# Edge lists read amid the second attention, root products behind it, and a front that works in node order

## The chip, the cores and the metric

The kernel runs on one core of a Trainium2 chip. The metric is the device time of one execution in microseconds (us). Before the change five executions took 2762.19 to 2769.22 us, with a median of 2766.24. Lower is better.

The core has four compute engines that run beside each other: TensorE (PE, matrix products), VectorE (DVE), ScalarE (ACT) and GpSimd (POOL). SyncE (SP) issues transfers. Indirect transfers (gathers and scatters of rows by an index list) are issued by POOL.

## The reference

A graph of 1250 nodes with 768 features and 20000 edges goes through two residual blocks. All is fp32.

```python
h = relu(layernorm(x))
# two GATv2 layers, 8 heads and then 1 head
fs = h @ Ws + bs ; fd = h @ Wd + bd
e = leaky_relu(fs[src] + fd[dst], 0.2)
alpha = softmax over the edges of one dst of einsum(e, attn)
out = elu(segment_sum(alpha * fs[src], dst))
# between them: h = layer_norm(out + h) * ln1_w + ln1_b
x = x + layer_norm(out of the second) * lno_w + lno_b

h = relu(layernorm(x))
# a relational layer over 34 edge types, then a graph convolution
seg = edge_type * n + dst
mean = segment_sum(h[src], seg) / max(count(seg), 1)
h1 = einsum('rni,rio->no', mean, W_rel) + h @ W_root + b_rgcn
xw = h1 @ W_gcn
dinv = rsqrt(deg + 1) ; norm = dinv[src] * dinv[dst]
x = x + segment_sum(xw[src] * norm, dst) + xw * dinv**2 + b_gcn
```

The edges arrive sorted by `dst`.

## The kernel before

**Order of the nodes.** Nodes are ranked by their number of incoming edges. A tile is 128 nodes of neighbouring rank; there are ten tiles (`NT`), and tile k has as many edge slots as its largest node needs (`CAPS[k]`, 33 in the first). A slot is one edge of each of the 128 nodes, so one indirect gather brings the 128 source rows of a slot. All slots of all tiles are 179.

**Front** (`fast_front`, L616 to L1076). It loads x, normalizes it, stores h (`f.h0_d`), and counts for each node where its edges begin in the sorted list (`got`, `first`, L777 to L829). `sources(j)` (L813 to L819) is the product h @ W1s of one block of rows; ten of them make the table `f.fs_d` that attention gathers from. Sort keys are spread over all partitions by products with `diag` (L859, L860); a comparison on DVE gives the `rank` (L865); ten scatters write the record (node, begin, degree) of each node to its rank's row (L880), and `rk` reads it back (L901). Then ten gathers fetch, for each rank, the window of the edge list that holds its edges (L912), and five select steps on DVE (L926 to L929) shift each window to its beginning; the result is `f.ell`. On PE's queue the shift product stands behind `sources(0)`, the key products behind `sources(1)`, and the others behind them.

`pairs` (`f.pairs`) computes for each edge how many edges of the same type its node has before it, and so which place the edge gets in the lists of the relations: DVE comparisons `same`, `cnt`, `early`, `turn` (L959 to L1030), counting products on PE (L970 to L979), a reduction over the partitions (`badc`, L1061, `fl_ps`, L1063), and `pick`/`pl` (L1024 to L1037). The places go to memory and come back as `f.place` (L1069, L1375).

**Attention** (`attention`, called twice). It works in chunks of up to 16 slots. `front(c, i)` gathers one slot into a ring of 24 buffers `fs` (L1148), optionally issues list scatters, and computes on DVE `z = max(fs, nfd)` (L1208), the product with the attention vector (L1213) and the sum per head (L1214); the one-head layer does the last two in one (L1210). `softmax` works on a chunk. `back` scales and sums the slots: with eight heads ACT scales (L1266) and PE adds with the identity (L1268), with one head ACT builds a diagonal matrix (L1256) and PE multiplies by it (L1258). While chunk j goes through `back`, chunk j+1 goes through `front`. At the end of a tile `end` divides, applies ELU and calls `finish`.

`list_edges` (called in `front`) issues scatters of the edge records into the lists `pair_d` of the relations (L1152), at 0.9 a slot from slot 16 of the first tile on, and 60 more at the last slot, or what is left of them. `negated1` gathers h of a tile, transposes it and multiplies it with W1d (L1116) for `nfd` (L1416). `finish1` normalizes, multiplies with the weights of the second layer (L1433, L1440) and scatters the table `fs2_d`. `finish2` normalizes, adds x, normalizes again, scatters h (`h2_d`), and computes the product with W_root, whose `root` rows (L1480) it scatters to `h1_d`.

**Relations.** After the second attention its pools are closed, and those of the relations opened. The lists are read (L1532), counts are made (L1536 to L1547, with one product, `more`, on PE), and then jobs run: `first_half` loads a relation's weights (L1159), gathers and sums the rows of its sources (`g`, `g2`, `g3`) and transposes them; `second_half` multiplies with the weights (L1116) and scatters with addition into `h1_d` (L1603). Beside that DVE writes an adjacency matrix (`arow`, L1511, L1513).

**Tail.** For some tiles the convolution is done by gathering and adding h1 rows (`acc`, `nb`, twelve buffers, L1665), for the others by products with the adjacency (L1674).

The order on each engine follows the program, save where `tc.issue_after` names an instruction that has to be issued first. A tile's buffer is waited for by its next user; a pool that is closed gives its memory to later pools, whose users wait for the last readers.

Of the kernel before, what the change touches and what calls it, by code (L numbers as in the profile page):

```python
# [18 lines left out]
P = 128  # L19
# [607 lines left out]
def fast_front(ctx, tc, f, x, src, dst, edge_type, W1s, b1s, W1d, b1d, attn1, attno, W_rel):  # L627
# [34 lines left out]
    rank_d = dram.tile([NP, 4], I32, name="f_rank_d")  # L662
# [9 lines left out]
    f.ell = keepp.tile([P, NT, S0], I32, name="f_ell")  # L672
# [4 lines left out]
    f.place_d = dram.tile([P, NT * S0], I32, name="f_place_d")  # L677
    f.w1d = const.tile([P, KC, D], F32, name="f_w1d")

    with ExitStack() as front:  # L680
# [110 lines left out]

        quarter = SLOPE / (1.0 - SLOPE)
# [29 lines left out]
        last = sources(0)  # L822
# [8 lines left out]
        with tc.issue_after(last.ins):  # L831
            last = nc.tensor.matmul(sh_ps[:, 0:1], shift, first[:, 0:1], start=True, stop=True)
        with tc.issue_after(last.ins):
            last = sources(1)
# [3 lines left out]


# [14 lines left out]
        with tc.issue_after(last.ins):  # L854
            for g in range(2):
                wide = ps_m.tile([P, 2, 512], F32, name="wide", tag="ag").rearrange("p a b -> p (a b)")
                for lo, hi in ((0, 512), (512, N // 2)):
                    at = slice(g * (N // 2) + lo, g * (N // 2) + hi)
                    nc.tensor.matmul(wide[:, lo:hi], ones16[:EP], flat2[:, at], start=True, stop=False)  # L859
                    last = nc.tensor.matmul(wide[:, lo:hi], big16[:EP], flat[:, at], start=False, stop=True)  # L860
                nc.scalar.copy(keys[:, g * (N // 2):(g + 1) * (N // 2)], wide[:, :N // 2])
# [7 lines left out]
        rec = prep.tile([P, NT, 4], I32, name="rec")  # L869
        nc.vector.memset(rec, 0)  # L870
        nc.vector.tensor_copy(rec[:, :, 0], node)
        nc.vector.tensor_copy(rec[:, :, 1], first[:, :NT])
        nc.vector.tensor_copy(rec[:, :, 2], deg)

        past = prep.tile([NP - N, 4], I32, name="past")
# [10 lines left out]
        with tc.issue_after(last_keys.ins):  # L886
            sources(2)


        packed = prep.tile([EP, EC], I32, name="packed")  # L890
        nc.vector.scalar_tensor_tensor(packed, ev[:, 2, :], 2048.0, ev[:, 0, :], op0=ALU.mult, op1=ALU.add)
        zrow = prep.tile([1, RW], I32, name="zrow")
        nc.vector.memset(zrow, 0)
        pk = packed.rearrange("p (r c) -> p r c", c=RW)
        nc.scalar.dma_start(win_d[1:NR + 1, :RW].rearrange("(p r) c -> p r c", p=EP), pk)
        nc.scalar.dma_start(win_d[0:NR, RW:].rearrange("(p r) c -> p r c", p=EP), pk)
        nc.scalar.dma_start(win_d[NR:NR + 1, RW:], zrow)


        rk = prep.tile([P, NT, 4], I32, name="rk")  # L900
# [3 lines left out]
        nc.vector.tensor_copy(f.degf, rk[:, :, 2])  # L904
        arow = prep.tile([P, NT], I32, name="arow")
        nc.vector.tensor_scalar(arow, rk[:, :, 1], 5, None, op0=ALU.arith_shift_right)
        nc.vector.tensor_scalar(arow, arow, float(NR - 1), 1.0, op0=ALU.min, op1=ALU.add)
        offs = prep.tile([P, NT], I32, name="offs")
        nc.vector.tensor_scalar(offs, rk[:, :, 1], RW - 1, None, op0=ALU.bitwise_and)
        win = prep.tile([P, NT, WIN], I32, name="win")  # L910
        for k in range(NT):
            nc.gpsimd.indirect_dma_start(  # L912
                out=win[:, k, :], out_offset=None, in_=win_d[:, :],
                in_offset=bass.IndirectOffsetOnAxis(ap=arow[:, k:k + 1], axis=0))
        wf = prep.tile([P, NT, WIN], F32, name="wf")
        nc.vector.tensor_copy(wf, win)
        bits = prep.tile([P, 5, NT], F32, name="bits")
        for i in range(5):
            bi = prep.tile([P, NT], I32, name="bi", tag="bi", bufs=2)
            nc.vector.tensor_scalar(bi, offs, i, 1, op0=ALU.arith_shift_right, op1=ALU.bitwise_and)  # L920
            nc.vector.tensor_copy(bits[:, i, :], bi)
        for i in (4, 3, 2, 1, 0):
            b = 1 << i
            L = S0 + b - 1
            df = prep.tile([P, NT, S0 + 15], F32, name="df", tag="df")
            nc.vector.tensor_sub(df[:, :, :L], wf[:, :, b:b + L], wf[:, :, :L])  # L926
            nc.vector.tensor_tensor(df[:, :, :L], df[:, :, :L],
                                    bits[:, i, :, None].to_broadcast([P, NT, L]), op=ALU.mult)
            nc.vector.tensor_add(wf[:, :, :L], wf[:, :, :L], df[:, :, :L])  # L929
        nc.vector.tensor_copy(f.ell, wf[:, :, :S0])  # L930
        nc.vector.tensor_scalar(f.srci, f.ell, 2047, None, op0=ALU.bitwise_and)
# [5 lines left out]
        def pairs():  # L937
# [13 lines left out]
            typ = pp.tile([P, NT, S0], I32, name="typ")  # L951
            nc.vector.tensor_scalar(typ, f.ell, 11, None, op0=ALU.arith_shift_right)
            tv = pp.tile([P, NT, S0], F16, name="tv")
            nc.vector.scalar_tensor_tensor(tv, pad, 100.0, typ, op0=ALU.mult, op1=ALU.add)
# [101 lines left out]
            pl_i = pp.tile([P, NT, S0], I32, name="pl_i")  # L1056
# [11 lines left out]
            nc.vector.scalar_tensor_tensor(pl_i, pad, float(P * COLS), pl, op0=ALU.mult, op1=ALU.add)  # L1068
            nc.sync.dma_start(f.place_d[:, :], pl_i.rearrange("p k s -> p (k s)"))  # L1069

        for j in range(3, NT):
            sources(j)
# [53 lines left out]
def fast_rest(ctx, tc, f, x, src, dst, edge_type, W1s, b1s, W1d, b1d, attn1, ln1_w, ln1_b,  # L1126
# [9 lines left out]
    h2_d = dram.tile([NP + P, D], F32, name="r_h2_d")  # L1136
    ZERO = NP + (PT + 1) * P
    h1_d = dram.tile([ZERO + 1, D], F32, name="r_h1_d")
    pair_d = dram.tile([P * f.COLS, 3], I32, name="r_pair_d")
# [11 lines left out]
    def scatter(table, rows, idx, group, **kw):  # L1151
        s = nc.gpsimd.indirect_dma_start(  # L1152
            out=table, out_offset=bass.IndirectOffsetOnAxis(ap=idx, axis=0), in_=rows, in_offset=None, **kw)
        tc.declare_no_dep(s.ins, group=group, reason="every node's row is written once")
        tc.add_to_no_dep_group(group, s.ins)

# [15 lines left out]
    def attention(H, table, negated, attn_e, first, loads, finish, rate, rest):  # L1172
# [21 lines left out]
        def front(c, i):  # L1194
# [5 lines left out]
            if s >= CHUNK or t.k:  # L1200
                list_edges(row, rate)
            if t.k == NT - 1 and s == t.S - 1:
                list_edges(row, rest)
            if t.lg is None:
                lg = pool.tile([P, S0 * f.H], F32, name="lg", tag="lg", bufs=2)
                t.lg = lg[:, :S0 * H].rearrange("p (s h) -> p s h", h=H)
# [116 lines left out]
        for j, now in enumerate(chunks):  # L1323
# [8 lines left out]
            if after:  # L1332
                softmax(after)
                if j + 2 == len(chunks):
                    for i in range(after.n):
                        back(after, i)
            if now.first + now.n == now.t.S:
                end(now.t)
# [10 lines left out]
    def prepare_lists():  # L1349
# [3 lines left out]
        with tc.tile_pool(name="r_fill", bufs=1, side="right") as fp:  # L1353
            lane = rp.tile([P, 1], F32, name="lane")
            nc.gpsimd.iota(lane, pattern=[[0, 1]], base=NP, channel_multiplier=1,
                           allow_small_or_imprecise_dtypes=True)
            fill = fp.tile([P, COLS, 3], I32, name="fill")
            nc.vector.memset(fill[:, :, 2], 0)
            ones_c = fp.tile([P, COLS], F32, name="ones_c")
            nc.vector.memset(ones_c, 1.0)  # L1360
            nc.vector.tensor_scalar(fill[:, :, 0], ones_c, lane, None, op0=ALU.mult)
            for t in range(PT + 1):
                cols = fill[:, :R * PC, 1].rearrange("p (r c) -> p r c", c=PC)[:, :, t] if t < PT else fill[:, R * PC:, 1]
                n = R if t < PT else PX
                nc.vector.tensor_scalar(cols, ones_c[:, :n], lane, float(t * P), op0=ALU.mult, op1=ALU.add)
            nc.vector.memset(fill[:, :R * PC, 1].rearrange("p (r c) -> p r c", c=PC)[:, :, PT:], 0)
            nc.sync.dma_start(pair_d.rearrange("(p c) f -> p c f", p=P), fill)
            zero = fp.tile([P, D], F32, name="zero")
            nc.vector.memset(zero, 0.0)
            nc.sync.dma_start(h2_d[NP:, :], zero)  # L1370
            for t in range(PT + 1):
                nc.sync.dma_start(h1_d[NP + t * P:NP + (t + 1) * P, :], zero)
            nc.sync.dma_start(h1_d[ZERO:, :], zero[:1])
        f.place = rp.tile([P, NT, S0], I32, name="place")
        nc.sync.dma_start(f.place, f.place_d.rearrange("p (k s) -> p k s", k=NT))  # L1375
# [21 lines left out]
    with ExitStack() as one:  # L1397
# [22 lines left out]
        def finish1(k, o):  # L1420
# [16 lines left out]
            scatter(fs2_d[:, :], fs, f.perm[:, k:k + 1], "fs2")  # L1437
# [6 lines left out]
        attention(H, f.fs_d, negated1, f.attn_1, prepare_lists, loads1, finish1, 0.9, 60)  # L1444
# [290 lines left out]
```

## Time and profile before

| What | us |
|---|---|
| median of five executions | 2766.24 |
| profiled execution, own time | 2764.64 |
| its span, first to last instruction | 2762.8 |
| front, to the first gather of h | 0 to 151.5 |
| first attention, first z to last table scatter | 183 to 884 |
| second attention, first gather to last sums | 888 to 1335 |
| last sums to the first relation product | 1335 to 1390 |
| relations | 1390 to 2561 |
| tail | 2561 to 2763 |

| Engine | busy us | share |
|---|---|---|
| PE | 2352.4 | 85% |
| DVE | 1566.3 | 57% |
| POOL | 1525.3 | 55% |
| ACT | 853.1 | 31% |

The mean granted TensorE clock was 0.933. The profile page shows one execution; its slices are 40 equal parts of the span, each digit the busy share in tenths. In the rows of the timeline the columns are start, busy time, engine, line, operation, output and inputs, and in brackets the idle time before it and what ended it. A busy share over the whole span hides the stages, so each stage is read by itself.

### The profile page before, as it was taken

The numbers are of one execution on the slowest core, as the hardware profiler recorded it, in microseconds if no ns is written. First come the engines' busy times: TensorE is split into PE (matmuls) and PEld (weight loads), VectorE is DVE, ScalarE is ACT, GpSimd is POOL, SyncE is SP. The second block draws the span as 40 slices with busy tenths as digits, with TensorE's granted clock in tenths as the row PEclk, the third lists the DMA queues.
The fourth block names the chain that finished last, engine by engine and source line by source line (L and its number), as shares of the span: only waits on it lengthen the run. The fifth ranks groups of instructions, "written<-read, shape, count | busy, mean of one in ns | idle before, by whom it ended". The sixth has DMA issues, their size and how long they took to land. (4 is left out here: it accounts for less than half of the span.)

```text
span 2762.8 us, 24188 instructions
## 1 busy us (share of the span) xinstructions
PE 2352.4 (85%) x7759; PEld 1364.5 (49%) x7759; DVE 1566.3 (57%) x2361; ACT 853.1 (31%) x2308; POOL 1525.3 (55%) x1113
## 2 busy tenths in 40 slices
PE   6953685788897486988699999999999999999688
PEld 3521243444454243544356666666666666665254
DVE  5599979998994999999362222222223232210262
ACT  3004766767862122333211112211212211222010
POOL 1343886878884776776275444444444454431471
PEclk8976897999998698999899999999999999999899
DMA  6155443445431776775387777777777777766783
GB/s 217 41 166 182 128 138 94 130 129 141 133 103 58 263 212 188 221 214 171 141 243 194 196 188 188 187 196 197 192 195 193 184 190 185 186 163 154 206 272 126
DMA packets 136549, 476.85 MB, mean 173 GB/s; under 512 B 26186, under 2 KB 28515, under 8 KB 136414
## 3 DMA queue, kind: packets, MB, share of 16 engines
q0 software_dynamic: 83712, 334.44, 46.8%
q1 hardware_dynamic: 48043, 134.21, 13.7%
q10 hardware_dynamic: 4658, 6.57, 0.7%
q8 instruction: 64, 1.05, 0.2%
q14 instruction: 72, 0.58, 0.1%
HBM read 385.91 MB, written 89.33 MB: 172 GB/s over the span
## 5 line engine op out<-in xcount | busy, mean ns | idle before, releaser
L1116 PE MATMUL ps<-wrel,mT 128*128 128x384 f32 x3336 | 1099.5, 486 | 1.5 <-DMA wrel<-in_L_gnn_W_rel_dram 1.5
L1116 PEld LDWEIGHTS ps<-wrel,mT 128*128 128x128 f32 x3336 | 623.3, 190 | 407.6 <-issue 1.5
L1148 POOL DMA_INDIRECT g<-r_h_d,lists x241 | 338.7, 1405 | 527.4 <-DVE g L1580 289.1
L1268 PE MATMUL ag<-fs,identf 128*128 128x384 f32 x716 | 286.3, 533 | 157.7 <-ACT fs L1266 147.6
L1580 DVE TENSOR_TENSOR g<-g,g 128x768 f32<-128x768 f32 x68 | 64.6, 950 | 612.7 <-DMA g<-r_h_d,lists 456.9
L1208 DVE TENSOR_TENSOR z<-fs,nfd 128x776 f32<-128x776 f32 (+1 forms) x358 | 351.2, 999 | 46.3 <-DMA fs<-f_fs_d,rec 25.6
L1266 ACT ACTIVATE fs<-fs,lg 128x96 f32<-128x96 f32 x1376 | 370.0, 363 | 0.3
L1258 PE MATMUL ag<-fs,dg 128*128 128x384 f32 x716 | 249.1, 508 | 81.9 <-ACT dg L1256 81.9
L1148 POOL DMA_INDIRECT fs<-f_fs_d,rec x179 | 246.2, 1376 | 95.4 <-issue 47.0
L1152 POOL DMA_INDIRECT r_pair_d<-rec,place x179 | 240.7, 1345 | 85.1 <-issue 42.7
L1148 POOL DMA_INDIRECT fs<-r_fs_d,rec x179 | 240.9, 1346 | 80.4 <-issue 31.6
L1603 POOL DMA_INDIRECT r_h_d<-y,lists x139 | 223.9, 1611 | 110.6 <-ACT y L1602 51.5
L1268 PEld LDWEIGHTS ag<-fs,identf 128*128 128x128 f32 x716 | 133.8, 202 | 298.3 <-ACT fs L1266 238.3
L1258 PEld LDWEIGHTS ag<-fs,dg 128*128 128x128 f32 x716 | 140.2, 199 | 187.4 <-ACT dg L1256 89.8
L1602 ACT ACTIVATE y<-ps,lists 128x768 f32<-128x768 f32 x71 | 64.1, 902 | 480.0 <-PE ps L1116 480.0
L1602 ACT ACTIVATE y<-ps,rcnt 128x768 f32<-128x768 f32 x68 | 61.4, 902 | 455.1 <-PE ps L1116 455.1
L1210 DVE SCALAR_TENSOR_TENSOR z<-z,attn_o 128x769 f32<-128x769 f32 x179 | 175.1, 996 | 0.6 <-ACT dg L1256 0.5
L1665 DVE TENSOR_TENSOR acc<-acc,nb 128x768 f32<-128x768 f32 x69 | 66.1, 958 | 187.9 <-DMA h<-r_h_d 133.4
L1213 DVE TENSOR_TENSOR z<-z,attn 128x776 f32<-128x776 f32 x179 | 168.3, 955 | 0.1
L1214 DVE TENSOR_REDUCE lg<-z 128x8 f32<-128x776 f32 x179 | 168.0, 950 | 0.1
L1513 DVE SCALAR_TENSOR_TENSOR arow<-node,from_f,arow 128x1250 f16<-128x1250 f16 x110 | 166.2, 1511 | 1.7
L1106 ACT COPY mT<-pt 128x384 f32<-128x384 f32 x278 | 119.2, 486 | 26.6 <-PE pt L1104 26.6
(283 smaller groups left out, 2290.3 us busy)
## 6 DMA issues: line engine op xcount, KB each, us to landing
wrel<-in_L_gnn_W_rel_dram SPq DMA_DIRECT2D x37, 2304.0 KB
g<-r_h_d,lists POOLq DMA_INDIRECT x241, 4.8
r_nfd_d<-fd SPq DMA_DIRECT2D x10, 384.0 KB
nfd<-r_nfd_d SPq DMA_DIRECT2D x10, 384.0 KB
r_x_d<-xb SPq DMA_DIRECT2D x10, 384.0 KB
x1r<-r_x_d SPq DMA_DIRECT2D x10, 384.0 KB
f_fs_d<-o_s SPq DMA_DIRECT2D x9, 388.0 KB
x<-in_x_dram SPq DMA_DIRECT2D x9, 384.0 KB
```

Source lines behind the costliest of these rows:

```text
L1116: last = nc.tensor.matmul(ps[:n, half, :f.HW], hT[:, k, j * P:j * P + n], w[:, k, cols], start=(k == 0), stop=(k == f.KC - 1 and not bias))
L1148: return nc.gpsimd.indirect_dma_start(out=to, out_offset=None, in_=table, in_offset=bass.IndirectOffsetOnAxis(ap=idx, axis=0))
L1152: s = nc.gpsimd.indirect_dma_start(out=table, out_offset=bass.IndirectOffsetOnAxis(ap=idx, axis=0), in_=rows, in_offset=None, **kw)
L1208: nc.vector.tensor_tensor(z, fs, t.nfd, op=ALU.max)
L1210: nc.vector.scalar_tensor_tensor(z[:, 0, :], z[:, 0, :], 1.0, attn_e[:, 0, :], op0=ALU.mult, op1=ALU.mult, accum_out=t.lg[:, s, :])
L1213: nc.vector.tensor_mul(z, z, attn_e)
L1214: nc.vector.tensor_reduce(t.lg[:, s, :], z, axis=AX.X, op=ALU.add)
L1258: nc.tensor.matmul(c.ps[:, half, :HW], dg, fs[:, 0, half * HW:(half + 1) * HW], start=begin, stop=end)
L1266: nc.scalar.activation(fs[:, h, :HD], fs[:, h, :HD], AF.Copy, scale=t.lg[:, s, h:h + 1])
L1268: nc.tensor.matmul(c.ps[:, half, :HW].rearrange("p (h d) -> p h d", d=HD), f.identf, fs[:, half * H // 2:(half + 1) * H // 2, :HD], start= ...
L1513: nc.vector.scalar_tensor_tensor(a, node16, from_f[:, k, s:s + 1], a, op0=ALU.is_equal, op1=ALU.add)
L1603: s = nc.gpsimd.indirect_dma_start(out=h1_d[:, :], out_offset=bass.IndirectOffsetOnAxis(ap=j.node, axis=0), in_=y, in_offset=None, compute ...
```

## The change

1. **Front in node order.** The windows are gathered and shifted in the order of the nodes, before the rank scatter. The scattered record of a node is (node, degree, 33 edges) instead of (node, begin, degree), and `f.typ` is taken from it instead of `f.ell`. The shift and key products stand ahead of all `sources`. The blank list and zero rows (`fill`, `zero`) and their stores move from `prepare_lists` into the front. `f.place` is written in place, with no way through memory.
2. **List scatters.** None before slot 23 of the first tile, 30 there, then 0.85 a slot, 4 at the last slot, and 7 and up to 40 behind the table scatters of tiles 7 and 8.
3. **Lists read in the second attention.** `read_lists` runs after `finish2(2)`, in a pool of its own.
4. **Ring given back at the last sums.** The root products of tiles 7, 8 and 9 are deferred. After the sums of tile 9 are issued, `give_back` issues that of tile 7 and closes the attention's pools; the relations' weight and row pools open there, the first job's first half follows, and then roots 8 and 9.
5. **Rest.** `nb` has 11 buffers, and the adjacency's DVE work is split out of `first_half` as `adjacency_slots`.

```diff
@@ fast_front
-    rank_d = dram.tile([NP, 4], I32, name="f_rank_d")
+    rank_d = dram.tile([NP, 2 + S0], I32, name="f_rank_d")
...
+        fill = prep.tile([P, COLS, 3], I32, name="fill")
+        nc.vector.memset(fill[:, :, 2], 0)
...
+        nc.sync.dma_start(f.pair_d.rearrange("(p c) f -> p c f", p=P), fill)
+        zero = prep.tile([P, D], F32, name="zero")
+        nc.vector.memset(zero, 0.0)
+        nc.sync.dma_start(f.h2_d[NP:, :], zero)
...
-        last = sources(0)
...
-        with tc.issue_after(last.ins):
-            last = nc.tensor.matmul(sh_ps[:, 0:1], shift, first[:, 0:1], start=True, stop=True)
-        with tc.issue_after(last.ins):
-            last = sources(1)
+        nc.tensor.matmul(sh_ps[:, 0:1], shift, first[:, 0:1], start=True, stop=True)
...
+        for j in range(NT):
+            nc.gpsimd.indirect_dma_start(
+                out=win[:EP, j, :], out_offset=None, in_=win_d[:, :],
+                in_offset=bass.IndirectOffsetOnAxis(ap=arow[:EP, j:j + 1], axis=0))
...
-        rec = prep.tile([P, NT, 4], I32, name="rec")
+        rec = prep.tile([P, NT, 2 + S0], I32, name="rec")
...
+        nc.vector.tensor_copy(rec[:EP, :, 2:], wf[:EP, :, :S0])
...
         with tc.issue_after(last_keys.ins):
-            sources(2)
+            sources(0)
...
-        for k in range(NT):
-            nc.gpsimd.indirect_dma_start(
-                out=win[:, k, :], out_offset=None, in_=win_d[:, :],
-                in_offset=bass.IndirectOffsetOnAxis(ap=arow[:, k:k + 1], axis=0))
...
-            nc.sync.dma_start(f.place_d[:, :], pl_i.rearrange("p k s -> p (k s)"))
...
-        for j in range(3, NT):
+        for j in range(1, NT):
             sources(j)
@@ attention
-            if s >= CHUNK or t.k:
+            if t.k == 0 and s == ring - 1:
+                list_edges(row, 30)
+            elif t.k or s >= ring:
                 list_edges(row, rate)
...
                 if j + 2 == len(chunks):
                     for i in range(after.n):
                         back(after, i)
+                    give_back()
@@ finish1
-            scatter(fs2_d[:, :], fs, f.perm[:, k:k + 1], "fs2")
+            row = scatter(fs2_d[:, :], fs, f.perm[:, k:k + 1], "fs2")
+            if NT - 4 < k < NT - 1:
+                list_edges(row, 7 if k < NT - 2 else 40)
...
-        attention(H, f.fs_d, negated1, f.attn_1, prepare_lists, loads1, finish1, 0.9, 60)
+        attention(H, f.fs_d, negated1, f.attn_1, prepare_lists, loads1, finish1, 0.85, 4)
@@ second attention
+    def give_back():
+
+        roots.pop(NT - 3)()
+        both.close()
+        f.consts.close()
...
+        late_hT = NT - 2 <= k
+        hT = (ap2 if late_hT else pool).tile([P, KC, P], F32, name="hT2", tag="hT2" if late_hT else "hT1",
+                                             bufs=2 if late_hT else 1)
         to_columns(nc, ps_t, f, hT, 0, h, P)
+
+        def root():
             ps, _ = dense(nc, ps_t, f, hT, late["wroot"], 0, P, tag="mm2", bias=(late["ones"], late["bias_r"]))
...
+        if k == 2:
+            read_lists()
+        if k < NT - 3:
+            root()
+        else:
+            roots[k] = root
...
+    def read_lists():
+
+        assert not edges
+        lists = rl.tile([P, COLS, 3], I32, name="lists")
+        nc.sync.dma_start(lists, pair_d.rearrange("(p c) f -> p c f", p=P))
...
+        nc.tensor.matmul(more[:, 0, :R], fold, is_edge[:, :, 2], start=True, stop=True)
+        nc.vector.tensor_add(rcnt[:, :, 0], rcnt[:, :, 0], more[:, 0, :R])
...
+    three = ExitStack()
+    wp = three.enter_context(tc.tile_pool(name="r_w", bufs=2))
+    gp = three.enter_context(tc.tile_pool(name="r_pair", bufs=1))
...
+    ahead = first_half(0)
+    for k in sorted(roots):
+        roots[k]()
+    two.close()
...
-    rq = ctx.enter_context(tc.tile_pool(name="r_late", bufs=1))
+    rq = ctx.enter_context(tc.tile_pool(name="r_late", bufs=1, side="right"))
...
-                g = gp.tile([P, D], F32, name="nb", tag="nb", bufs=12)
+                g = gp.tile([P, D], F32, name="nb", tag="nb", bufs=11)
```

## The prediction

> **What bounds the kernel now.** I read the 40 slices of the page first, then the busy time per stage, then the timeline at the joints between the stages. The slices show one engine after another at the limit:
>
> ```profile
> PE   6953685788897486988699999999999999999688
> DVE  5599979998994999999362222222223232210262
> POOL 1343886878884776776275444444444454431471
> PEclk8976897999998698999899999999999999999899
> ```
>
> PE fills the front, DVE both attentions (slices 5 to 18, with POOL close behind), PE the relations.
>
> ```profile
> 200.00:250.00 50.00, 6.14 (x14) 3.09 (x13) 49.82 (x74) 6.15 (x20) 3.44 (x4) 0.57 0.54 196
> ...
> 890.00:1335.00 445.00, 338.02 (x990) 187.86 (x989) 417.05 (x791) 132.92 (x272) 313.15 (x224) 0.88 0.66 207
> 1335.00:1392.00 57.00, 28.55 (x89) 16.00 (x88) 20.04 (x36) 10.62 (x15) 20.38 (x17) 0.73 0.55 211
> 1392.00:2560.00 1168.00, 1166.51 (x4201) 718.43 (x4200) 315.53 (x277) 235.64 (x462) 546.88 (x368) 1.00 0.74 188
> ```
>
> The busy columns are PE, PEld, DVE, ACT, POOL. In 200–250 DVE has no gap and POOL works 3.44 us of 50. In 1335–1392 nobody is busy half the time: a chain sets that stretch. From 1392 PE is busy 1166.5 of 1168. So time is to be had before 1392, and a microsecond saved there stays saved. The chain, from the timeline:
>
> ```profile
> 1320.93 14.46 PE L1258 MATMUL ag<-fs,dg 128*128 128x384 f32 x44
> ...
> 1335.43 1.02 DVE L1274 TENSOR_SCALAR att_o<-ag,den 128x768 f32<-128x768 f32 x1 [10.37 <-PE ag L1258]
> ...
> 1350.37 0.97 POOL L1152 DMA_INDIRECT r_h_d<-h,f_perm  x1 [0.17 <-DVE hT L1108]
> ...
> 1362.80 0.97 POOL L1152 DMA_INDIRECT r_h_d<-root,f_perm  x1 [0.56 <-ACT root L1480]
> 1370.47 0.32 SPq L1532 DMA_DIRECT2D lists<-r_pair_d  x1
> ...
> 1374.43 0.97 POOL L1148 DMA_INDIRECT g<-r_h_d,lists  x1 [10.65 <-DMA lists<-r_pair_d]
> ...
> 1382.97 0.96 DVE L1580 TENSOR_TENSOR g<-g,g 128x768 f32<-128x768 f32 x1 [7.12 <-DMA g<-r_h_d,lists]
> ...
> 1390.31 2.16 PE L1116 MATMUL ps<-wrel,mT 128*128 128x384 f32 x5
> ```
>
> The last sums start only when the root product of tile 7 has left PE; the last h goes out at 1350.37; the list load goes 20 us after it, and the first gather waits for that load.
>
> **The change, part by part.** The profiled execution took 2764.64 (span 2762.80), 1.60 under the median 2766.24.
>
> *Transition, deferred roots and early lists: −22 (−12 to −28).* Root(7)'s products, two halves of 4.14 + 0.91, go behind the sums of tile 9. These can start after the softmax at 1313.1, at about 1314.5; eleven slots at ACT's 1.29 us (its rows stand 1.29 apart) end at 1329, 6.4 earlier. Root(7) then holds PE 10.1 us, and tile 9's DVE chain now has the copies of tile 8's h columns in front of its add, so it waits for root(7): to about 1339.5. From that add (1343.61) to h's end (1348.74) is 5.1, so h is there at 1344.6 and goes out at 1345 (before: 1350.37). A gather that depends on a scatter started 4.27 after it (883.57 to 887.84): first gather 1349 instead of 1374.43. From gather to first transposes was 12.95 (1374.43 to 1387.38): 1362. PE has meanwhile root(8) and most of root(9); one half of that (5.1) and the second job's transposes lie before the first relation product: about 1368, against 1390.31. The first weights must be there: their load may start when the ring's memory comes back, 1329 to 1343, and 2304 KB at the 211 GB/s of that stretch takes 11 us, 20 when shared: 1363 at the latest. Ends: without the earlier sums −15.6, with a late weight load −12; with nothing behind g −28. POOL's two root scatters now lie between gathers (0.98 + 0.30 each), SP's weight load no longer behind the list load.
>
> *Lists in the second attention: +2 (0 to +4).* Eight small DVE instructions, 2.0 us in all by the same lines at 1373–1376, go into a DVE that is busy 417 of 445; the load itself goes behind wroot's, on an SP with little to do.
>
> *Front in node order: −5 (−8 to +9).* Windows are gathered at about 50 instead of 103.85 and picked on DVE before the rank scatter, so the pair work starts near 107 instead of 128 and its `early`/`turn` part (15 us) lies under PE. But `sources` now starts behind the key products: near 54.5 plus some 2 us of slow clock, against 48.77. Its ten steps of 9.9 are back to back, so PE's end goes from 146.76 to about 154 and the first gather from 151.46 to 159. Against that, the reduction that ended the pair work (169.07) comes at 166.4, as it now only follows the counting products, the dense product behind it at 168 and nfd at 178 instead of 181.54 (−3); and `fill`, `ones_c` and `zero`, 2.5 us of DVE at 214.80–217.19, leave a DVE without gaps (−2.5). Their 2.3 MB join a DMA at 0.82 in the first 50 us. If the pair work is not what held nfd, the whole PE delay shows: +9. A window gather per node order costs POOL the same ten issues.
>
> *Lists' burst in the first attention: −4.3 (−16 to +28).* 30 scatters go out at once where POOL is idle behind a full ring, from the places' end, near 206, and the 37 at the end (796 to 852.90) vanish: they held one fs2 scatter and, through its buffer, L1433 at 856.08, whose product was there at 854.8: −1.3. In the steady state some 7 fewer scatters are left of 1.3 to 2.6 us; DVE's waits for gathers there are 25.6 us in all:
>
> ```profile
> POOL fs L1148 <- PE ag L1268: 40.1, 24, 25.7
> DVE z L1208 <- DMA fs<-f_fs_d,rec: 25.6, 21, 4.5
> ```
>
> (engine, line, releaser: us, times, longest). I take −3. What a scatter costs beside DVE the trace shows twice, with the same three DVE operations running:
>
> ```profile
> 221.90 0.99 POOL L1152 DMA_INDIRECT r_pair_d<-rec,place  x1 [0.30 <-DVE z L1208]
> 223.20 0.97 POOL L1152 DMA_INDIRECT r_pair_d<-rec,place  x1 [0.31 <-issue]
> ...
> 254.82 3.64 POOL L1148 DMA_INDIRECT fs<-f_fs_d,rec  x1 [0.30 <-issue]
> ...
> 407.01 2.35 POOL L1152 DMA_INDIRECT r_pair_d<-rec,place  x1 [0.30 <-issue]
> ```
>
> 1.30 per scatter in one phase, 2.65 in another. At 1.30 the burst ends at 245, when the first ring buffer comes free (249.87 before, about 244 now): hidden. At 2.65 it ends at 285; DVE, which first ran out at 266.68, less 6, then stands until the gathers land, some 4 us later: +28. I take 1.30, the row at the same place. The Trainium skill ("GPSIMD Engine Reference", 1. Specifications) says that POOL's SBUF interface is shared with VectorE and contended by instructions with two SBUF inputs; z and the multiplication are such. By it the slow row would be the rule and the sum would be 28 us higher; the rows at 220 show that it need not be.
>
> *Tail: +1 (0 to +3).* nb has 11 buffers for 12; DVE released POOL there 8 times for 2.4 us in all, and the gathers' own landing sets the pace (18.7 us of waits).
>
> The relations' 1168 us stay: PE alone sets them. Sum: −22 + 2 − 5 − 4.3 + 1 = −28.3, so 2736.3 for the profiled execution, and 2738 against the median.
>
> **Rivals.**
> - *The burst locks at 2.65 us.* For it: 404–436, where each issue takes one DVE period of 2.62. Against: 220–224. −28.3 + 28 gives 2766; half of the burst locked 2752.
> - *The front gives nothing:* PE's later end shows in nfd, +6 in place of −5: 2749.
> - *The transition does not do what it says:* pools or weights come late and the first product stays within 10 us of 1390: 2750.
> - *Slower:* the burst runs as the gathers of 249–264 did, 3.64 + 0.30 each: 118 us from 206, so the ring is refilled from 324 and DVE stands from 260 to 328, +68, of which POOL's lighter load later returns some 10: 2796. It decides for slower when a scatter of the burst takes over 3.0 us on average (206 + 30 × 3.0 = 296, 34 more than the 262 that costs nothing).
>
> **How the numbers follow.** This kernel tells 0.2% (5.5 us) from no change. Chances: the forecast's case 0.50 (2720 to 2745), burst wholly or half locked 0.18, front without gain 0.12, transition late 0.10, slow burst 0.06, several of the small losses beyond their bounds 0.04. Predicted 2738. Low end: transition −28, front −8, attention −10 gives 2721; high end: full lock, 2766 with 2 on top. Faster takes the first, 13 of the second's 18, the front and transition cases: 0.83; same 0.07; slower 0.10.
>
> **What the profile after would show.** Right: first relation product near 1340 (1368 less the gains before it); 30 scatters 1.30 apart between 206 and 245 with the first ring gather at once behind them; the first softmax operation (241.60) near 236; no run of list scatters at the end of the first attention; no load of lists in the transition. Wrong: a scatter mean of 2.6 there and DVE waiting for a gather near 260–290; `sources` ending past 156; PE waiting for `wrel` before its first product; POOL waiting for `nb` buffers in the tail.

## The result, and the profile after

The changed kernel took 2768.91 us (median of 26 executions) against 2765.37 for the kernel before (47 executions): a ratio of 1.0009, with a 95% interval of 1.0000 to 1.0018. Nothing was gained, where 28 us had been forecast. The profiled execution took 2768.11, its span is 2766.3, 3.5 longer than before. In one of the later series of runs ("three edits" the first time, "transition alone", "roots at once", "no multiplication") the kernel before took 2784.96 and not some 2766, so the times of that series are compared only with this one.

The 40 slices of the page after:

```profile
PE   4874484888998467889899999999999999999687
DVE  7658779999996799999563222222222222210262
POOL 3137777777872675778365444454444454431471
PEclk7986797999999788999999999999999999999899
```

PE is less busy in the first two slices (4 and 8 for 6 and 9) and again in the fifth, POOL busier in the fourth (7 for 3). The busy time by stage (PE, PEld, DVE, ACT, POOL):

```profile
100.00:150.00 50.00, 40.18 (x110) 20.43 (x110) 34.74 (x88) 4.45 (x11) 3.28 (x3) 0.90 0.14 45
150.00:200.00 50.00, 37.55 (x150) 19.75 (x149) 25.31 (x59) 5.47 (x14) 19.27 (x18) 0.88 0.46 150
200.00:250.00 50.00, 10.58 (x30) 6.18 (x30) 50.00 (x63) 2.24 (x3) 36.97 (x20) 0.60 0.66 222
250.00:400.00 150.00, 95.39 (x228) 40.02 (x229) 119.04 (x174) 109.64 (x400) 121.66 (x94) 0.83 0.39 105
...
1335.00:1392.00 57.00, 49.25 (x149) 27.21 (x147) 20.15 (x39) 19.62 (x33) 24.74 (x21) 0.91 0.53 189
1392.00:2560.00 1168.00, 1166.49 (x4204) 718.57 (x4203) 320.79 (x284) 236.91 (x465) 552.19 (x371) 1.00 0.74 190
```

In 100 to 150, PE was busy 49.1 us before and is busy 40.2 now. In 200 to 250, POOL works 37 us in place of 3.4. In 250 to 400, DVE is busy 119.0 in place of 127.7. A few points of the timelines say where the time went:

| Point | before | after | shift |
|---|---|---|---|
| end of the last source product (PE) | 146.8 | 170.8 | +24.1 |
| first nfd (DVE) | 181.5 | 193.6 | +12.0 |
| last gather of the first attention | 794.0 | 813.9 | +20.0 |
| first gather of the second attention | 887.8 | 910.7 | +22.8 |
| division of tile 9 (its sums are done) | 1335.4 | 1354.6 | +19.2 |
| first list gather of the relations | 1374.4 | 1376.6 | +2.2 |
| first relation product | 1390.3 | 1393.9 | +3.6 |
| end | 2762.8 | 2766.3 | +3.5 |

The front lost 12 us, the first attention 10.8, the way from there to the first relation product gained 19.3, and from there on nothing changed (1372.5 and 1372.4). So the gain that carried the forecast is there, and two losses, together a little larger, ate it.

**The transition**, from the timeline after:

```profile
1338.56 16.03 PE L1278 MATMUL ag<-fs,dg 128*128 128x384 f32 x44
...
1354.63 1.02 DVE L1294 TENSOR_SCALAR att_o<-ag,den 128x768 f32<-128x768 f32 x1 [6.70 <-PE ag L1278]
...
1369.25 0.96 POOL L1168 DMA_INDIRECT r_h_d<-h,f_perm  x1 [1.52 <-ACT h L1482]
...
1376.58 0.98 POOL L1164 DMA_INDIRECT g<-r_h_d,lists  x1 [6.37 <-issue]
...
1383.04 0.96 DVE L1565 TENSOR_TENSOR g<-g,g 128x768 f32<-128x768 f32 x1 [11.74 <-DMA g<-r_h_d,lists]
...
1394.52 1.04 POOL L1168 DMA_INDIRECT r_h_d<-root,f_perm  x1 [0.58 <-ACT root L1492]
```

The list load is gone from between the scatter of h and the first gather, and from the division of tile 9 to that gather it is 22.0 us in place of 39.0 (the rows before, 1335.43 and 1374.43, stand in the prediction). The last root scatter (1394.52) now lies behind the first relation product.

**The front**, first four rows of the kernel before:

```profile
48.77 6.28 PE L813 MATMUL ps<-w1s,hT 128*128 128x388 f32 x12
...
103.32 0.30 ACT L1377 ACTIVATE dinv<-f_degf,f_ones_col 128x10 f32<-128x10 f32 x1 [14.92 <-DVE f_degf L904]
...
145.87 0.89 PE L814 MATMUL ps<-bias,ones_row 1*98 1x388 f32 x2
...
181.54 0.96 DVE L1416 SCALAR_TENSOR_TENSOR nfd<-ps,bias 128x768 f32<-128x768 f32 x1 [0.25 <-PE ps L1116]
```

and then the timeline after:

```profile
58.05 6.09 PE L839 MATMUL ps<-w1s,hT 128*128 128x388 f32 x12 [0.16 <-ACT keys L905]
...
98.73 0.91 PE L840 MATMUL ps<-bias,ones_row 1*128 1x388 f32 x2
...
105.52 0.37 SPq L949 DMA_DIRECT2D rk<-f_rank_d  x1
...
108.70 0.30 ACT L1375 ACTIVATE dinv<-f_degf,f_ones_col 128x10 f32<-128x10 f32 x1 [27.95 <-DVE f_degf L952]
108.91 0.78 ACT L843 COPY o_s<-ps 128x768 f32<-128x768 f32 x1
...
109.82 5.81 PE L839 MATMUL ps<-w1s,hT 128*128 128x388 f32 x12 [10.17 <-ACT o_s L844]
...
169.95 0.89 PE L840 MATMUL ps<-bias,ones_row 1*98 1x388 f32 x2
...
193.57 0.96 DVE L1414 SCALAR_TENSOR_TENSOR nfd<-ps,bias 128x768 f32<-128x768 f32 x1 [0.76 <-PE ps L1135]
```

The first full half block of source rows starts at 58.05 in place of 48.77. Later PE stands 10.17 us for ACT's copy of a source block. ACT stood 27.95 us before that, at `dinv`: the square root of the degrees needs the ranks that were read back, and it stands on ACT's queue ahead of the copies. In the kernel before it stood there too, idle for 14.92 us until 103.32; PE did not stop for it. The last source product ends 24.1 us later than before, which is about what three terms make together: the later start, 9.3; the stall, 10.2; and 4.9 for a half block that PE had done ahead of 48.77 in the kernel before.

**The burst of list scatters**, POOL and DVE side by side:

```profile
227.04 2.29 POOL L1168 DMA_INDIRECT r_pair_d<-rec,place  x1 [0.30 <-issue]
227.51 0.95 DVE L1228 TENSOR_TENSOR z<-fs,nfd 128x776 f32<-128x776 f32 x1
228.38 0.94 DVE L1234 TENSOR_REDUCE lg<-z 128x8 f32<-128x776 f32 x1
229.25 0.94 DVE L1233 TENSOR_TENSOR z<-z,attn 128x776 f32<-128x776 f32 x1
229.63 2.29 POOL L1168 DMA_INDIRECT r_pair_d<-rec,place  x1 [0.30 <-issue]
...
282.34 0.97 POOL L1168 DMA_INDIRECT r_pair_d<-rec,place  x1 [0.30 <-issue]
283.62 0.97 POOL L1168 DMA_INDIRECT r_pair_d<-rec,place  x1 [0.30 <-issue]
284.89 1.00 POOL L1164 DMA_INDIRECT fs<-f_fs_d,rec  x1 [0.30 <-PE ag L1288]
```

and DVE's waits in 180 to 300:

```profile
DVE z L1228 <- DMA fs<-f_fs_d,rec: 19.2, 1, 19.2
```

(The columns are those of the prediction's wait lines: us, times, longest.) From 224 to 250 a scatter takes one whole period of DVE's three operations, 2.62 us; near the end, with DVE at a stand, 1.28. The 30 need 60.5 us, the ring is refilled at 284.89, and DVE stands 19.2 us. Over the whole first attention DVE's waits for gathers come to 39.9 us, against 25.6 before.

### The profile page after: what moved, and what is told of

Read it like the earlier page. It is cut to its first block, busy times and chain, and to the rows that moved or that the text cites. A ratio compares the mean times of both kernels' runs of the same rounds, so it can differ in the third digit from the quotient of the medians.

```text
span 2766.3 us, 24164 instructions
## 1 busy us (share of the span) xinstructions
PE 2359.5 (85%) x7759; PEld 1368.6 (49%) x7759; DVE 1560.9 (56%) x2360; ACT 853.0 (31%) x2308; POOL 1540.0 (56%) x1113
## 5 line engine op out<-in xcount | busy, mean ns | idle before, releaser
L1228 DVE TENSOR_TENSOR z<-fs,nfd 128x776 f32<-128x776 f32 (+1 forms) x358 | 343.5, 976 | 59.7 <-DMA fs<-f_fs_d,rec 39.9
L1168 POOL DMA_INDIRECT r_pair_d<-rec,place x179 | 255.1, 1425 | 61.9 <-issue 45.2
L1164 POOL DMA_INDIRECT fs<-f_fs_d,rec x179 | 237.8, 1329 | 79.7 <-issue 48.7
L1123 PEld LDWEIGHTS pt<-identf,g 128*128 128x128 f32 x834 | 99.8, 141 | 47.4 <-issue 24.5
```

Of the source, the lines that this page charges most:

```text
L1164: return nc.gpsimd.indirect_dma_start(out=to, out_offset=None, in_=table, in_offset=bass.IndirectOffsetOnAxis(ap=idx, axis=0))
L1168: s = nc.gpsimd.indirect_dma_start(out=table, out_offset=bass.IndirectOffsetOnAxis(ap=idx, axis=0), in_=rows, in_offset=None, **kw)
L1228: nc.vector.tensor_tensor(z, fs, t.nfd, op=ALU.max)
```

## The experiments

My theory after the result: (a) the front loses by PE, which starts its source blocks later and then stops behind `dinv` on ACT; (b) the burst is slowed by DVE's operations with two inputs, comes too late to refill the ring, and costs the first attention about 11 us; (c) the transition is worth 20 us by itself. Rivals: the stores of the blocks wait on SP behind the load of the ranks; the attention's loss comes from elsewhere; the transition gained only because the kernel arrived there late.

The table gives the stages of every run in its profiled execution: first nfd, from there to the first gather of the second attention, from there to the first relation product, and the span.

| Run | nfd | first attention | second attention and transition | span |
|---|---|---|---|---|
| before | 181.5 | 706.3 | 502.5 | 2762.8 |
| after | 193.6 | 717.1 | 483.2 | 2766.3 |
| dinv late | 182.9 | 713.4 | 482.6 | 2748.8 |
| pace of before | 195.4 | 703.6 | 485.4 | 2758.1 |
| burst of 12 | 194.3 | 699.1 | 484.5 | 2751.6 |
| block 0 first | 176.8 | 715.7 | 485.2 | 2751.8 |
| three edits | 177.5 | 706.7 | 482.9 | 2742.5 |
| three edits again | 177.0 | 705.7 | 484.9 | 2741.6 |
| blocks 0 and 1 first | 175.8 | 702.6 | 484.6 | 2733.8 |
| transition alone | 191.0 | 719.1 | 482.8 | 2763.2 |
| transition, burst of 12 | 182.4 | 710.2 | 482.9 | 2745.6 |
| roots at once | 194.4 | 723.9 | 485.5 | 2779.9 |
| no multiplication | 196.5 | 710.4 | 483.0 | 2762.4 |

Each row is one execution. In the column of the second attention and transition all rows but the first lie between 482.6 and 485.5, so a difference of 2 or 3 us between two rows of it tells little.

**dinv late.**

```diff
-            nc.scalar.copy(ov[:n, :, :, HD], ps[:n, :, HW:QW])
+            f.last_copy = nc.scalar.copy(ov[:n, :, :, HD], ps[:n, :, HW:QW])
...
-        nc.scalar.activation(f.dinv, f.degf, AF.Sqrt, bias=f.ones_col, scale=1.0)
+        with tc.issue_after(f.last_copy.ins):
+            nc.scalar.activation(f.dinv, f.degf, AF.Sqrt, bias=f.ones_col, scale=1.0)
```

> The changed kernel, with one order added: ACT computes dinv only after the last copy of a source block. Theory (dinv, which waits for the ranks read back, stands on ACT's queue ahead of the copies of source blocks 2 to 9, and PE has two PSUM buffers only): the 10.17 us stall of PE at 109.82 goes, the last source product ends near 159 instead of 170.8, nfd comes near 182 instead of 193.6, and the whole is 10 to 12 us shorter, about 2757. Rival (the stores of the blocks wait on SP behind the load of the ranks, and the three o_s buffers run out): the stall stays at about 10 us, and the time at 2769.

2759.48, ratio 0.9979 (0.9967 to 0.9991): 9 us less than the changed kernel. The profiled execution (2750.63) is the fastest of twelve, so its span in the table shows more gain than the median. From its timeline:

```profile
101.57 4.18 PE L839 MATMUL ps<-w1s,hT 128*128 128x388 f32 x12
101.72 0.80 ACT L843 COPY o_s<-ps 128x768 f32<-128x768 f32 x1 [9.07 <-issue]
...
160.07 0.89 PE L840 MATMUL ps<-bias,ones_row 1*98 1x388 f32 x2
161.79 0.32 ACT L1376 ACTIVATE dinv<-f_degf,f_ones_col 128x10 f32<-128x10 f32 x1
...
182.92 0.95 DVE L1415 SCALAR_TENSOR_TENSOR nfd<-ps,bias 128x768 f32<-128x768 f32 x1
```

PE runs through, the last source product ends at 161.0 and nfd comes at 182.92, 10.7 sooner. The SP rival falls: the load of the ranks still stands ahead of the stores, and no source product waits for it. The `dinv` that was computed so early is needed by nobody before the first list scatter, at 213.71.

**Pace of before.**

```diff
-            if t.k == 0 and s == ring - 1:
-                list_edges(row, 30)
-            elif t.k or s >= ring:
+            if s >= CHUNK or t.k:
                 list_edges(row, rate)
...
-            if NT - 4 < k < NT - 1:
-                list_edges(row, 7 if k < NT - 2 else 40)
...
-        attention(H, f.fs_d, negated1, f.attn_1, prepare_lists, loads1, finish1, 0.85, 4)
+        attention(H, f.fs_d, negated1, f.attn_1, prepare_lists, loads1, finish1, 0.9, 60)
```

> The changed kernel with the list scatters paced as before: 0.9 a slot from slot 16 on, the rest at the last slot, none behind the table scatters. Theory (30 scatters at once run at 2.62 us each beside DVE and refill the ring too late): DVE's wait of 19.2 us at the first refill goes, the last gather of the first attention comes about 8 us sooner against nfd, and the whole is 7 to 11 us shorter, 2758 to 2762. Rival (the attention's loss comes from another thing than the burst, such as PE's order at its end): under 3 us shorter, 2766 to 2769.

2759.83, ratio 0.9987 (0.9973 to 1.0002). The first refill comes at 261.21, DVE's waits for gathers in the first attention fall from 39.9 to 22.7 us, and that stage takes 703.6 in place of 717.1. So the burst is the loss of the first attention. In the whole time it is 9 us by the medians and 6 by the ratios, whose intervals just touch (1.0000 to 1.0018 for the changed kernel); the next run shows it more clearly.

**Burst of 12.**

```diff
-                list_edges(row, 30)
+                list_edges(row, 12)
...
-finish1, 0.85, 4)
+finish1, 0.92, 4)
```

> The changed kernel with 12 scatters at slot 23 instead of 30, and then 0.92 a slot. Theory: 12 at 2.62 us are 31 us from 224 on, so they end near 256, before the first ring buffer comes free near 259; DVE waits under 3 us there, and the whole is 8 to 12 us shorter, 2757 to 2761. Rival (any burst there costs its own length, since POOL would be short of time anyway): shorter by 12 us only where 18 scatters less mean so, but a wait of some 8 us stays at the refill, 2763.

2753.08, ratio 0.9955 (0.9941 to 0.9970), 15 us by the ratios and a little better than expected. POOL at the refill:

```profile
251.29 1.64 POOL L1168 DMA_INDIRECT r_pair_d<-rec,place  x1 [0.30 <-issue]
253.24 1.74 POOL L1168 DMA_INDIRECT r_pair_d<-rec,place  x1 [0.30 <-issue]
260.08 3.35 POOL L1164 DMA_INDIRECT fs<-f_fs_d,rec  x1 [5.10 <-PE ag L1288]
```

The twelfth ends at 255, POOL waits 5.10 us for the buffer, and DVE's waits there are 2.8 us (2.5 in the kernel before), over the stage 25.8. So here a burst that ended before the first buffer came back cost nothing that can be seen.

**Block 0 first**, with dinv late; the key products, too, are ordered behind block 0:

```diff
+        last = sources(0)
         gotf = prep.tile([P, NT, RW], F32, name="gotf")
...
-        nc.tensor.matmul(sh_ps[:, 0:1], shift, first[:, 0:1], start=True, stop=True)
+        with tc.issue_after(last.ins):
+            last = nc.tensor.matmul(sh_ps[:, 0:1], shift, first[:, 0:1], start=True, stop=True)
...
         with tc.issue_after(last_keys.ins):
-            sources(0)
+            sources(1)
...
-        for j in range(1, NT):
+        for j in range(2, NT):
             sources(j)
```

> The changed kernel with dinv late and with source block 0 ahead of the shift and key products, as before the change; the windows stay in node order. Theory (the front's loss is PE's later start, 9.3 us, the half block that PE no longer does while it waits for weights, 4.9, and the stall, 10.2; the node order itself gains 12): the last source product ends near 149, nfd comes near 172, 21 us sooner than in the changed kernel, and the time is about 2748. Rival (with the keys later the ranks come later, and the pair work on DVE ends behind PE): nfd near 180, 2756.

2753.58, ratio 0.9957 (0.9941 to 0.9973). nfd comes at 176.8: 6 us sooner than with dinv late alone, where 11 were expected. The last source product ends at 154.9, not 149: PE stands 3.98 us until 51.83 for the bias row, which it had at 47.19 before (on DVE's queue the wait for the gathered edge rows stands ahead of it in both kernels, and ends at 50.60 in place of 45.96), and 2.1 us around the keys. Why the edge rows came later was not tried.

**No multiplication.** The product with the attention vector is left out and a second reduction stands in its place. The kernel then computes something else; it was run once, for its trace.

```diff
-                nc.vector.tensor_mul(z, z, attn_e)
+                nc.vector.tensor_reduce(t.lg[:, s, :], z, axis=AX.X, op=ALU.max)
                 nc.vector.tensor_reduce(t.lg[:, s, :], z, axis=AX.X, op=ALU.add)
```

> The changed kernel with the multiplication by the attention vector (heads of the first attention) left out and a second reduction put in its place, so DVE's three operations keep their time (z with two inputs, and two reductions with one input) and the logits are others. Theory (POOL's issue of a scatter stands still while DVE runs an operation with two inputs from SBUF and goes on beside a reduction): of 2.62 us now 1.75 are open instead of 0.87, so two scatters fit into a period, the burst's scatters come 1.3 us apart beside a busy DVE, it ends near 264, and DVE's wait at the first refill is under 5 us. Rival (any busy DVE slows POOL, or the distance is that of the transfers): still 2.6 apart and 19 us of wait.

A part of the burst's timeline:

```profile
231.16 1.01 POOL L1168 DMA_INDIRECT r_pair_d<-rec,place  x1 [0.30 <-issue]
231.25 0.95 DVE L1234 TENSOR_REDUCE lg<-z 128x8 f32<-128x776 f32 x1
232.12 0.95 DVE L1233 TENSOR_REDUCE lg<-z 128x8 f32<-128x776 f32 x1
232.47 0.98 POOL L1168 DMA_INDIRECT r_pair_d<-rec,place  x1 [0.31 <-issue]
232.99 0.95 DVE L1228 TENSOR_TENSOR z<-fs,nfd 128x776 f32<-128x776 f32 x1
233.76 1.03 POOL L1168 DMA_INDIRECT r_pair_d<-rec,place  x1 [0.30 <-issue]
```

and its DVE waits:

```profile
DVE z L1228 <- DMA fs<-f_fs_d,rec: 2.6, 3, 1.5
```

DVE is as full as in the changed kernel, with the same three times of 0.95, and the first 26 scatters come 1.31 apart on average. So it is not a busy DVE as such that slows POOL, and not the transfers; it is what DVE runs. (The first attention is only 6.7 us shorter, 710.4: this run has two gaps of DVE of 9.3 and 7.5 us for which the trace names no instruction or transfer.) In the changed kernel a scatter that starts within the multiplication (229.63) ends 2.29 later, at the end of the next reduction (231.00 to 231.94). That fits a work of 0.97 us that begins only when the two operations with two inputs are over. The Trainium skill ("SBUF — State Buffer", Who interferes with whom) states such a rule: a VectorE instruction with two SBUF inputs contends with a GpSimd instruction that reads SBUF; one with at most one, outside VectorE's two-port modes, does not. The burst agrees. What it does not explain by itself is the kernel before at 223.20, where a scatter took 0.97 almost wholly beside z (223.25 to 224.21), started 0.05 ahead of it; how a scatter comes to start in the favourable phase stays open.

**Three edits together** (dinv late, block 0 first, burst of 12), run in two series:

> The changed kernel with dinv late, source block 0 ahead of the keys, and 12 scatters at slot 23 with 0.92 a slot after it: the edits of two earlier runs together. Theory (the front's loss and the burst's are separate and lie one behind the other on the path): nfd near 177 as in the run with block 0 first, the first refill of the ring near 243, and the two gains add: 15 and 16 us under the changed kernel's 2769, 2738. Rival (they overlap, since a burst that starts earlier ends earlier too): 2745 to 2750.

2749.73 against 2784.96, ratio 0.9873 (0.9840 to 0.9906).

> The combined edits once more, for the kernel before took 0.7% longer than usual in the series in which they were run first. Theory: 0.990 to 0.993 of the kernel before (the sum of the three single gains: front 15, burst 16, less the changed kernel's 2). Rival: 0.987, as in that series, if the new front is spared something that the old one suffers.

2743.42 against 2764.50, ratio 0.9914 (0.9898 to 0.9930). The gains add: the two single edits took 0.0052 and 0.0054 off the changed kernel's 1.0009, which makes 0.990, within the interval.

**Transition alone.** The kernel before with parts 3 and 4, its front and pace untouched; the diff is that of the second attention and the relations above, without the front, `list_edges` and `finish1`.

> The kernel before with parts 3 and 4 alone (lists read in the second attention, root products deferred, the ring given back at the last sums, relation pools opened there), and 11 nb buffers; the front and the scatters' pacing stay as before. Theory (the transition is worth what the two traces show between the last softmax and the first relation product, 20 us): 2746, with the first list gather some 22 us after the last sums instead of 39. Rival (the transition gained only since the changed kernel arrives there late, with lists long landed and weights early): under 10 us, 2756 or more.

2764.69 against 2784.96, ratio 0.9920 (0.9895 to 0.9945), 22 us. From the first gather of the second attention to the first relation product it takes 482.8 in place of 502.5. In every run with this transition, on early and on late arrival, the stage takes 482.6 to 485.5: the rival falls.

**Roots at once.**

```diff
-        roots.pop(NT - 3)()
         both.close()
...
-        if k < NT - 3:
-            root()
-        else:
-            roots[k] = root
+        root()
```

> The changed kernel with every root product issued at once in its tile, as before; the ring is still given back at the last sums and the lists are read early. Theory (the early lists are worth some 15 of the 20 us, the deferred products the rest): 5 to 8 us longer than the changed kernel, 2774 to 2777, with the sums of tile 9 starting some 5 us later behind root 7. Rival (the deferral is worth nothing, since root 7's wait only moves behind the sums into tile 9's chain): within 2 us of 2769.

2778.02 against 2784.96, ratio 0.9971 (0.9949 to 0.9993). Its stage takes 485.5, 2.3 longer than in the changed kernel and at the edge of what the other runs have. Its span is 13.6 longer, of which 6.8 lie in the first attention (723.9) and 3.7 behind the first relation product, neither of which this edit touches. The division of tile 9 comes 10 us later (453.9 after the first gather of the second attention, against 444.0), the first relation product stands 31.5 behind it in place of 39.3. So the rival is nearly right: deferring moves root 7 from one side of the last sums to the other, and most of the gain of 19 is that of the early lists and pools, which were not tried apart.

**Blocks 0 and 1 first**, on the three edits:

```diff
+        with tc.issue_after(last.ins):
+            last = sources(1)
...
         with tc.issue_after(last_keys.ins):
-            sources(1)
+            sources(2)
...
-        for j in range(2, NT):
+        for j in range(3, NT):
             sources(j)
```

> The kernel of the combined edits, with source block 1 too ahead of the key products, as before the change. Theory (with block 0 alone ahead, PE still idles some 3 us around the keys, whose inputs come from DVE): the last source product ends near 150 instead of 154, nfd comes near 173, and the time is 3 to 4 us under that of the combined edits. Rival (the ranks then come 5 us later, and the pair work on DVE, which had 8 us to spare, ends later than PE): nfd at 177 or later, no gain.

2735.44, ratio 0.9891 (0.9876 to 0.9907): 29 us under the kernel before, and the best of all. From its timeline:

```profile
151.82 0.89 PE L840 MATMUL ps<-bias,ones_row 1*98 1x388 f32 x2
...
175.83 0.95 DVE L1420 SCALAR_TENSOR_TENSOR nfd<-ps,bias 128x768 f32<-128x768 f32 x1
...
1321.90 1.02 DVE L1299 TENSOR_SCALAR att_o<-ag,den 128x768 f32<-128x768 f32 x1 [6.70 <-PE ag L1283]
1344.02 0.98 POOL L1169 DMA_INDIRECT g<-r_h_d,lists  x1 [6.53 <-issue]
```

nfd is only 1 to 2 us sooner than with block 0 alone, not 4: PE still waits 3.77 us for the bias row. The rest of its lead over the three edits (2743.42) lies in the first attention, 702.6 for 705.7, and behind the first relation product, 1370.8 for 1374.1, neither of which this edit aims at; that part is not explained, and the intervals of the two ratios overlap.

**Transition with a burst of 12**, on the front of before:

```diff
-            if s >= CHUNK or t.k:
+            if t.k == 0 and s == ring - 1:
+                list_edges(row, 12)
+            elif t.k or s >= ring:
                 list_edges(row, rate)
...
+            if NT - 4 < k < NT - 1:
+                list_edges(row, 7 if k < NT - 2 else 40)
...
-finish1, 0.9, 60)
+finish1, 0.92, 4)
```

> The kernel before with parts 3 and 4 and with the scatters paced 12 at slot 23, 0.92 a slot and the rest behind the table scatters, but the front as before the change. Theory (the node order is worth 4 us once its start and its stall are mended, and the small burst is worth what it took from the end, 4 to 8): 2739 to 2742 where the kernel before has 2766, 4 us longer than the combined edits. Rival (the front of before is as good): the same time as the combined edits.

2746.07, ratio 0.9927 (0.9914 to 0.9941), where 2739 to 2742 were expected. Against the three edits with the mended node-order front (2743.42) that is 2.7 us, which the intervals do not tell from nothing, against the best front 10.6. By nfd it is 4.9 to 6.5. So the node order is worth some 5 us in nfd once it is mended, and the small burst by itself nothing that can be told: the first attention took 699.1 to 710.2 with it in five runs (mean 704.9), 703.6 and 706.3 with the pace of before in two, 719.1 in a third (transition alone). With the burst of 30 it took 713.4 to 723.9 in four (mean 717.5): 12 us more than with 12.

## Why the prediction was wrong

The time, 2768.9, lies just above the range (2721 to 2768), and the forecast gain did not come. Two steps failed, that of the front and that of the burst. By the steps:

- *Transition, −22:* right in sum; 19.3 in the trace, 19.7 in the stage of the run with it alone. Its parts are off both ways, so that the sum came out so near is in part luck: the last sums gained 4.7 and not 6.4 (16.03 us for eleven slots, not 14.2), the scatter of h came 14.6 after them and not 16, the first gather 7.3 behind it and not 4.3, the transposes 10.4 behind that and not 12.95. What I credited to the deferral is worth 2 at most.
- *Lists in the second attention, +2:* right; the stage to the division took 444.0 against 447.6, with the 4.7 of the sums in it, which leaves +1.1.
- *Front, −5:* wrong, +12. The step that failed is "Its ten steps of 9.9 are back to back, so PE's end goes from 146.76 to about 154". It went to 170.8. I had counted the later start (58.05 against 48.77), but not that PE before had used its waits for weights to do half a block, 4.9 us, nor the 10.17 of stall. The sum behind PE's end was right: 24 us to nfd, and 22.7 measured, so the node order did what it was to do there. I moved the rank scatter past PE and POOL and did not ask which queue waits for the ranks: ACT, at an instruction far from the diff.
- *Burst, −4.3:* wrong, +10.8. The step is "I take 1.30, the row at the same place". It ran at 2.62 for the first ten and 2.02 on average, and DVE stood 19.2; the other row, of 407, was the right one for these, and the bound of +28 held. The burst also began at 224.36, when the places were there, and not near 206. The rule of the skill that I set aside there agreed with the burst. What the 37 scatters at the end had cost could not be told from nothing.
- *Tail, +1:* within its bounds; relations and tail took 1372.4 against 1372.5, though POOL waited for DVE 15 times (7.3 us) in place of 8 (2.4).
- *Rivals:* "the burst locks" (2766) and "the front gives nothing" (2749) both came true at once, the second worse than priced. I gave each a chance as if they excluded each other; they lie one behind the other and add.
- *Slips in the sums:* the cases that I counted as faster add up to 0.85, not 0.83 (0.05 are left for "same"); the low end is 2721 from the profiled execution and 2723 from the median; and PE's 28.55 of 57 us in 1335 to 1392 is just half, not under it. None of them decides anything.

## What to carry to other kernels

When a step is moved, look for every queue on which something waits for its result, far from the diff too: an instruction without haste, such as a square root for a later stage, can hold the copies that a busy engine depends on, and an order behind the last of them cost nothing here. Work that POOL does in a gap of its own is free only if it ends before the gap does. Where a trace has two prices for the same issue, as here 1.30 and 2.62 us beside VectorE operations with two inputs, a burst whose length decides is to be priced at the higher one until a run has shown the lower. Gains and losses of stages that lie one behind the other add, so rivals in different stages have to be summed, not chosen between.

## What the runs showed of the hardware

- The length of an indirect scatter's issue beside a full VectorE depends on what VectorE runs: 2.29 to 2.37 us beside max, reduction and multiplication (ten in a row, in the changed kernel), 0.97 to 1.13 beside max and two reductions (26 in a row), with VectorE's times of 0.95 the same.
- In the profile of "transition alone", VectorE was busy 4.35 of 10 us in 170 to 180, against 9.65 in the kernel before, in gaps for which the trace names VectorE's own instructions, "issue" or once "remote", while the transfer engines were busy 0.89 (0.84 before); nfd came at 191.0 in place of 181.5. What lengthens the gaps was not tried.
